# Four graph layers on one core: layer 3's transposes through DRAM rewritten, the last graph's end cut in two, and a new instruction order

## The chip, the cores and the metric

The kernel runs on one core of a Trainium2 chip. Its metric is the device time of one execution, in microseconds. The engines named below are TensorE (PE, with PEld for its weight loads), VectorE (DVE), ScalarE (ACT), GpSimd (POOL) and SyncE (SP), which here issues every DMA.

## The reference

There are 64 graphs of 256 tokens with 256 features each, and a 256 x 256 adjacency per graph, all in fp32. Four layers follow each other, and each ends with `x = layernorm(x + layer(x, adj))`.

```python
# layer 0: 4 heads of 64
X, q, k = lrelu(x @ W_lin + b_lin), lrelu(x @ W_q), lrelu(x @ W_k)      # slope 0.01, split into heads
adj_h = adj * sigmoid(q @ k.T / 8); deg = adj_h.sum(-1)
dis = where(deg > 0, deg ** -0.5, 0)
Y = (dis[:, None] * adj_h * dis[None, :]) @ X                           # then a layernorm with ln_g, ln_b
# layer 1: 8 heads of 32
q, k, v = x @ Wq + bq, x @ Wk + bk, x @ Wv + bv
out = softmax(where(adj > 0, q @ k.T / sqrt(32), NEG)) @ v              # per head, then @ Wo + bo
# layer 2
agg = epsilon * x + adj @ x
h = silu(rmsnorm(agg @ W1 + b1) * rms_weight)                           # 256 -> 1024
out = h @ W2 + b2
# layer 3: one head
Wh = x @ W; e = lrelu(Wh @ a1 [:, None] + Wh @ a2 [None, :])            # slope 0.2
h = softmax(where(adj > 0, e, NEG)) @ Wh
out = gelu(layernorm(h) * gamma + beta)
```

## The kernel before

**Tiles.** A tile has 128 partitions. A graph's 256 x 256 matrix is held as 128 x 512, two blocks of 128 rows side by side. An fp32 matmul of 128 x 128 weights with 128 x 256 data appears in the trace as a pair of PE instructions; a product of two 256 x 256 matrices takes four such matmuls. Heads use small tiles of TensorE: layer 0's scores (L550) have 64 rows, layer 1's (L631) 32 rows; layer 0's product AX (L590) fills 64 columns at a time, and layer 1's attention times values `av` (L667), the degrees `deg` (L568) and the mean of squares of layer 2 (L733) 32 columns. The planner calls these modes `rows` and `columns`, and the others `full` and `transpose`.

**One graph after another, interleaved.** The function `graph` writes down the operations of one graph. Each is recorded by `Plan.op` with its engine, a cost, the values that it reads and writes, a delay `after` until its result has landed, and, for a DMA, a size. `Plan.order` then runs a greedy list scheduler over the operations of all 64 graphs: it keeps a clock for each engine, and takes next the ready operation with the smallest key.

```python
key = start + LEAD[op.rank], op.due + RANK[op.rank], op.graph, op.index
```

`LEAD` and `RANK` have one number per operation of a graph, `CHANGE` is the cost of going from one PE mode to another, `STAY` and `TURN_STAY` bias against leaving the small-tile modes, `AHEAD` limits how early a graph starts, and `SLOTS` is the number of buffers of each kind. Activation tables are taken in turns (`ROUND`, `TAIL`), so that a graph's layer 1 runs two turns after its layer 0, and so on: several graphs are in flight, each in another layer. `JOINT` glues the mean-of-squares matmul of one graph to a score matmul of another. The engines' instructions are issued in the order that this plan gives; nothing is reordered on the chip.

**Transposes.** TensorE needs the contracted index on the partitions, so tokens and features change places several times. Most of these transposes go through DRAM: DVE transposes 32 x 32 blocks (L377), SP writes the tile to a DRAM buffer `far` (64 KB pieces at L383), and reads it back with the blocks in their new places (L387). Layer 0 uses the form with `in_order=False` (one write of 256 KB at L391, four reads at L393), layer 1 a similar one (L652 to L656), and layer 3 the form with `in_order=True`, twice a graph: for its input `xT3` and for its attention weights `eT`. In the first and last graphs (`NEAR`) TensorE transposes instead (L365), and one ACT copy of 128 x 512 (L412) brings the result out of PSUM.

**Layer 3 and the end.** The input is transposed, multiplied by the weights with two more columns for a1 and a2 (L770), copied (L774), and one of the extra columns is spread over the partitions as a row (`row_of`, L402 to L405: DVE and four POOL operations). ACT adds and applies the leaky relu (L778), the softmax is L513 on DVE and L518 on ACT, `eT` is the transposed weights, and `token_major` (L432) multiplies them with the values. Statistics are L445 to L457 with one power on POOL (L455); then L490 to L504 scale and shift, L789 is the gelu, L790 the sum with x, a second normalisation gives `o` (L464 to L472), and L792 writes 256 KB out. For the last three graphs (`ENDS`) ACT does part of the scaling (L493, L468).

Of the kernel before, what the change touches and what calls it, by code (L numbers as in the profile page):

```python
# [9 lines left out]
AF = mybir.ActivationFunctionType  # L10
# [19 lines left out]
AHEAD = 12.7  # L30
STAY, TURN_STAY = 197, 988
# [8 lines left out]
SLOTS = {"s": 42, "d": 10, "b": 3, "c": 72, "p": 8, "h": 8, "t": 5, "w": 3, "f": 8}  # L40
# [3 lines left out]
    3.44, -1.34, 0, 0.79, 3.63, 0, 7.06, 0, 0, 2.3, -1.09, 0.34, 2.1, 0.78, 0.47, 0, -8.07, 0, -2.5, 0, 15.95,  # L44
    3.93, 0.83, -0.82, -4.23, -2.95, 1.61, -7.35, 4.27, 6.06, 1.96, 5.09, -16.2, 5.57, 0.49, -0.6, 0, 0.29, 0.2,
    0, 8.07, 0, 0.26, 0, 0, -8.02, -0.52, 0.34, -5.71, 0, 1.06, -2.37, 0.99, -8.94, 0, 0, -4.56, -2.34, -6.61,
    0.36, 0.84, -1.13, 0.53, 4.6, -1.2, -1.71, 0, 0, 0, -0.62, 4.15, -3.45, -2.5, -0.12, 6.63, 0.18, 0, 0.38,
    -0.79, -2.84, 0, -12.65, 1.3, 0, -1.96, 1.34, -1.62, 20.11, -1.52, 0, -0.8, -2.32, -1.64, 0, -1.22, -15.66,
    0, -6.95, -2.98, 0, 0.05, -1.56, -0.82, -0.77, -6, -2.56, -2.91, -11.65, -5.25, -1.35, -5.62, 0.33, 0, 0.59,
    -0.44, -28.89, -6.83, 0, 0.4, 0, 0.46, 0.76, 0, 0, 12.94, -5.14, 4.78, 3.27, 0.41, -2.4, -1.34, 0, -0.87,  # L50
    -1.92, 0, -2.52, 0, -10.08, -2.01, 3.32, 0.57, -18.67, -3.41, 0, 4.56, 5.08, 3.05, -3.62, 0, 3.39, -0.48,
    -0.64, -0.1, -3.66, 19.76, -6.53, 16.91, 0, -3.84, -1.2, 0.37, -12.68, 0, -6.52, 5.03, 11.31, 6.22, 1.25,
    -5.4, 5.28, 9.76, 2.05, -0.81, -6.1, 0.74, -0.33, -6.78, -1.35, 0.27, 2.67, -2.73, 0.77, -0.98, -12.61, 0,
    1.81, 1.44, 1.4, -0.43, -5.6, 1.17, 0, -3.52, -0.14, -0.86, -0.05, -0.51, 0, 25.51, 0, 0, 0, -2.88, 0, 0, 0,
    -0.4, -0.07, 0, 0, 2.29, 0, 0, -2.22, -0.14, 1.6, 0.52, -0.32, -2.95, 0, 0, 0, -0.56, 0, -0.75, 8.73, 0, 0,
    0, 0.27, 9.58, -7, 0.78, 1.68, 0, -0.23, -10.25, -9.94, 0, 2.37, 3.11, -1.12, 0.31, -0.32, 0, -2.88, -2.04,
    0, -2.34, -0.49, -1.73, -1.73, -3.1, -1.77, 1.2, -3.97, 0.04, -0.58, -3.77, -19.26, 1.61, 0, 2.15, 0, 1.75,
    -9.45, 0, -11.3, -4.22, -40.55, -11.19, -1.7, 0, -1.02, 20.28, 2.54, 0, 0, -11.95, -3.71, 4.81, 4.78, 0, 1.6,
    0, 0, 0, -4.09, 0, -20.33, 0.55, 0.76, 0, 0, -5.26, 0.23, 2.23, 0.95, 0.44, -0.83, -0.57, -4.63, -0.68,
    -0.52, 11.56, 0.73, 0, 0, 5.95, 1.53, -1.94, 0, 1.27, 0.18, 0, -0.41, -3.03, -5.78, -1.03,  # L60
# [3 lines left out]
    0, 0, 0, 4, 0, 21, 963, 0, 0, 0, 63, 0, 36, -156, 0, 241, -51, 5, -54, -409, 0, 480, 0, -31, 0, 0, -1244, 5,  # L64
    0, 581, -13, 104, -75, 53, 0, 0, 0, 0, 0, 0, 0, 0, 0, 0, 0, 100, 0, 0, 0, 0, -88, -216, 0, -127, 0, 0, 0, 0,
    0, 0, 0, 0, 0, 0, 0, 0, 0, 0, 0, 0, 0, 73, 0, -648, -13, 0, 0, 0, 0, 0, 243, 0, 0, 0, 0, 0, 0, 52, 0, 0, 0,
    0, 0, 0, 0, 0, 0, -1022, -191, 0, 0, 0, -79, 0, 13, -157, 0, 0, 0, 0, 0, 0, 0, 0, 0, 0, 0, 0, 0, 0, 0, 0, 0,
    0, -14, -96, -46, -142, 175, -7, -49, -988, -8, 0, 0, 0, 0, -3, 56, -31, 223, 0, 72, -40, -885, 811, -10, 0,
    0, 0, 0, -181, 559, -5, 0, 0, 323, 144, 0, 239, -109, 0, 0, -40, 0, -97, -886, 230, 144, -105, 0, 2, -92, 38,
    -275, 0, 0, 0, 0, 0, -262, 0, 0, 0, -468, -319, 0, 0, 0, 0, -390, 256, 267, 0, 0, 0, 0, 0, 42, 0, 0, 0, 0, 0,  # L70
    -325, 0, 0, 0, 0, 0, -236, 0, -117, -279, 0, 0, -1, 0, 0, 0, 0, 0, 0, 0, 0, -14, 0, 0, 0, 0, 0, 0, 0, 0, 0,
    0, 0, 0, 0, 0, 0, -261, -256, 0, 0, 0, 0, 0, 0, 0, 0, -139, 0, 0, 37, 0, 0, 0, 0, 0, -156, 0, 0, 0, 0, 0, 0,
    0, 0, 0, -25, 0, 262, -10, 105, 0, 0, 0, 0, 0, -34, -107, -53, -189, -141, -364, 0, 0, -161, -46, -115, 0,
    -12, 0, -883, 0, 0, 0, 0, 0, 0, -109, -14, 0, 187, 0, -13, 721, 0, 0, -68, -68, 0, -58, 0, -31, 417, 0, 227,
]

# [40 lines left out]
class Plan:  # L117
# [66 lines left out]
    def order(self):  # L184
# [17 lines left out]
        while ready:  # L202
            best = None
            for op in ready:
# [10 lines left out]
                for kind, n in need.items():  # L215
                    free = self.free[kind]
                    if len(free) < n:
                        break
                    start = max(start, sorted(free)[n - 1][0])
                else:  # L220
                    key = start + LEAD[op.rank], op.due + RANK[op.rank], op.graph, op.index
                    if best is None or key < best[0]:
                        best = key, start, op
# [116 lines left out]
def graph(plan, nc, c, t, out, b):  # L340
# [14 lines left out]
    def load(name, src):  # L355
        v = Value("s", name, 2)
        op("SP", 470, lambda: nc.sync.dma_start(two(v), t[src][b].rearrange("(n p) d -> p n d", p=P)), [v], after=5000, size=256)
        return v
# [14 lines left out]
    def far_transposed(src, name, in_order=True):  # L373


        eb, far, dst = Value("s", "eb"), Value("h", "far", 4), Value("s", name, 4)
        op("DVE", 635, lambda: dve.transpose(  # L377
            eb.t.rearrange("p (b g i) -> p g b i", b=4, i=32),
            src.t.rearrange("p (n k w) -> p k n w", n=2, k=2)), [eb], [src])
        if in_order:  # L380
            F = lambda a: far.t[:64].rearrange("(a z) (y w) -> a (z y) w", a=4, w=P)[a]
            for a in range(4):
                op("SP", 470, lambda a=a: nc.sync.dma_start(  # L383
                    F(a).rearrange("(b j) w -> j b w", b=4),
                    eb.t[32 * a:32 * a + 32].rearrange("j (b w) -> j b w", b=4)), [(far, a)], [eb], after=2400, size=64)
            for a in range(4):
                op("SP", 655, lambda a=a: nc.sync.dma_start(  # L387
                    dst.t.rearrange("q (g a i) -> a q g i", g=4, a=4)[a],
                    F(a).rearrange("q (g i) -> q g i", g=4)), [(dst, a)], [(far, a)], after=2200, size=200)
            return dst  # L390
        op("SP", 470, lambda: nc.sync.dma_start(far.t[:, :512], eb.t), [(far, i) for i in range(4)], [eb], after=2900, size=256)  # L391
        for q in range(4):
            op("SP", 470, lambda q=q: nc.sync.dma_start(  # L393
                dst.t[32 * q:32 * q + 32].rearrange("j (a g) -> j a g", a=4),
                far.t[:, :512].rearrange("(a j) (b g) -> b j a g", a=4, b=4)[q]), [(dst, q)],
                [(far, i) for i in range(4)], after=1900, size=64)
        return dst

    def row_of(column, src, name):

        blocks, row = Value("t", "blocks"), Value("w", name, 4)
        op("DVE", 110, lambda: dve.transpose(  # L402
            blocks.t.rearrange("p (n k) -> p n k", n=NB), column().to_broadcast([P, NB, 32])), [blocks], src)
        for a in range(4):
            op("POOL", 300, lambda a=a: pool.partition_broadcast(  # L405
# [20 lines left out]
    def token_major(xT, w, r=()):  # L426

        ps = Value("p", "ps", 2)
        for n in range(NB):
            def fn(n=n):  # L430
                for k in range(DB):
                    pe.matmul(two(ps)[:, n, :], two(xT)[:, k, n * P:(n + 1) * P], w()[:, k, :],  # L432
# [7 lines left out]
    def stats(src, r=None):  # L440
# [13 lines left out]
        op("DVE", 300 if r else 60, fn, [mv], [mv] + [r] * bool(r))  # L454
        op("POOL", 720, lambda: pool.tensor_tensor(m()[:, :, 0], m()[:, :, 0], c.mhalf[:, :NB], OP.pow), [mv], [mv], after=400)  # L455
# [71 lines left out]

    xT, adjT, x, adj = load("x0T", "xT"), load("adjT", "adjT"), load("x", "x"), load("adj", "adj")
# [43 lines left out]
    op("DVE", 340, lambda ps=ps: dve.transpose(pd.t[:, :N], ps.t[:, :N]), [pd], [ps])  # L572
# [3 lines left out]
    op("POOL", 1610, lambda: pool.tensor_tensor(dp.t[:, :8], dp.t[:, :8], c.mhalf, OP.pow), [dp], [dp])  # L576
# [20 lines left out]
    else:  # L597
        yb = far_transposed(ps, "yT", in_order=False)
# [25 lines left out]
    for hq in range(H1 // 4):  # L624
# [9 lines left out]
        for pair in range(2):  # L634
# [20 lines left out]
            for q in range(4):  # L655
                op("SP", 470, lambda far=far, eT=eT, q=q: nc.sync.dma_start(  # L656
# [17 lines left out]
    op("DVE", 110, lambda: dve.transpose(  # L674
        rT.t.rearrange("p (n k h) -> p n k h", n=NB, h=H1),
        r.t[:, :16].rearrange("p (n h) -> p n h", n=NB)[:, :, None, :].to_broadcast([P, NB, 4, H1])), [rT], [r])
    op("SP", 470, lambda far=far: nc.sync.dma_start(far.t, rT.t), [far], [rT], after=2000, size=32)
    for h in range(H1):
        op("SP", 470, lambda h=h, far=far: nc.sync.dma_start(
            two(rb)[h % 4 * HD1:(h % 4 + 1) * HD1, h // 4, :].rearrange("p (a m) -> p a m", a=4),  # L680
            far.t.rearrange("(a c) m -> c a m", a=4)[h][None].to_broadcast([HD1, 4, 64])),
            [(rb, h)], [far], after=2000, size=40)
# [55 lines left out]
    op("DVE", 125, lambda ps=ps: dve.transpose(pm(), ps.t[:, :64]), [(sq, 1)], [ps])  # L738
    op("DVE", 50, lambda: dve.tensor_scalar(  # L739
        rs.t[:, :NB], pm().rearrange("p (n k) -> p n k", k=32)[:, :, 0], 1e-6, None, op0=OP.add), [rs], [(sq, 1)])  # L740
    op("POOL", 700, lambda: pool.tensor_tensor(rs.t[:, :NB], rs.t[:, :NB], c.mhalf[:, :NB], OP.pow), [rs], [rs])  # L741
# [19 lines left out]
    xT3 = copy(transposed(x), "xT3") if b >= plan.graphs - NEAR[2] else far_transposed(x, "xT3")  # L761
# [3 lines left out]
    for n in range(NB):  # L765
        ps = Value("p", "ps")

        def fn(ps=ps, n=n):
            for k in range(DB):
                pe.matmul(ps.t[:, :D + 2], two(xT3)[:, k, n * P:(n + 1) * P], c.w3.t[:, k, :],  # L770
# [6 lines left out]
    for n in range(NB):  # L777
        op("ACT", 360, lambda n=n: act.activation(two(e)[:, n, :], s2.t, AF.Prelu, bias=s1(n), alpha=0.2),  # L778
# [104 lines left out]
```

## Time and profile before

| what | value |
|---|---|
| median of 3 runs | 2665.98 us (2665.81 to 2669.04) |
| the profiled execution | 2665.97 us, its span 2664.2 us |
| PE busy | 2629.6 us, 99% |
| DVE busy | 2463.8 us, 92% |
| ACT busy | 2246.5 us, 84% |
| POOL busy | 640.5 us, 24% |
| share of the 16 DMA engines taken by packets | 69.7% |
| TensorE clock granted, mean | 0.996 of full speed |

The span is the time from the first to the last instruction in the trace; what is outside it is the difference to the profiled execution's own time. "Busy" is the time in which an engine carries out instructions. A wait is charged to the engine that waited, with what released it. A period is the distance between the same work of two consecutive graphs; 64 of them overlap.

### The profile page before, as it was taken

The numbers are of one execution on the slowest core, as the hardware profiler recorded it, in microseconds if no ns is written. First come the engines' busy times: TensorE is split into PE (matmuls) and PEld (weight loads), VectorE is DVE, ScalarE is ACT, GpSimd is POOL, SyncE is SP. The second block draws the span as 40 slices with busy tenths as digits, with TensorE's granted clock in tenths as the row PEclk, the third lists the DMA queues.
The fourth block names the chain that finished last, engine by engine and source line by source line (L and its number), as shares of the span: only waits on it lengthen the run. The fifth ranks groups of instructions, "written<-read, shape, count | busy, mean of one in ns | idle before, by whom it ended". The sixth has DMA issues, their size and how long they took to land.

```text
span 2664.2 us, 54927 instructions
## 1 busy us (share of the span) xinstructions
PE 2629.6 (99%) x17248; PEld 2122.6 (80%) x17248; DVE 2463.8 (92%) x6905; ACT 2246.5 (84%) x5343; POOL 640.5 (24%) x1029
## 2 busy tenths in 40 slices
PE   8999999999999999999999999999999999999997
PEld 6777888888887888888888878878888887877786
DVE  6799999999999999999999999999999999989976
ACT  4888888888888888988888888889889888888886
POOL 1122222222222222222222222222222222222222
PEclk9999999999999999999999999999999999999998
DMA  4577777776777777777767777777677776676761
GB/s 142 153 210 199 196 206 188 200 202 182 210 195 187 197 200 192 200 189 200 200 187 206 196 186 202 196 188 200 193 195 203 188 199 183 178 198 186 212 162 38
DMA packets 764628, 502.48 MB, mean 189 GB/s; under 512 B 383792, under 2 KB 724144, under 8 KB 764336
## 3 DMA queue, kind: packets, MB, share of 16 engines
q1 hardware_dynamic: 764336, 498.97, 69.7%
q8 instruction: 137, 2.24, 0.4%
q14 instruction: 155, 1.27, 0.2%
HBM read 301.35 MB, written 197.39 MB: 187 GB/s over the span
## 4 chain that ended last, share of the span: by engine, by line
PE 89%; DVE 5%; DMA 2%; SPq 1%; issue 1%; ACT 1%; POOL 1%; POOLq 0%; DVEq 0%; ACTq 0%
PE ps L432 16%; PE ps L755 15%; PE ps L421 15%; PE ps L714 15%; PE ps L631 5%; PE ps L702 4%; PE ps L550 4%; PE ps L590 4%; PE av L667 4%; PE ps L770 4%; PE ps L365 1%; PE ps L568 1%; DVE mv L445 1%; DVE e L513 1%; DMA eT<-far 1%
## 5 line engine op out<-in xcount | busy, mean ns | idle before, releaser
L518 ACT ACTIVATE e<-e,low 128x256 f32<-128x256 f32 x1152 | 576.4, 503 | 156.9 <-DVE low L513 150.9
L455 POOL TENSOR_TENSOR mv<-mv,mhalf 128x2 f32<-128x2 f32 x384 | 313.7, 822 | 965.7 <-DVE mv L453 759.8
L714 PE MATMUL ps<-aggT,w 128*128 128x256 f32 x2048 | 463.8, 379 | 0.0
L755 PE MATMUL ps<-w,hT 128*128 128x256 f32 x2048 | 456.4, 380 | 0.0
L755 PEld LDWEIGHTS ps<-w,hT 128*128 128x128 f32 x2048 | 387.8, 190 | 56.1 <-issue 2.7
L714 PEld LDWEIGHTS ps<-aggT,w 128*128 128x128 f32 x2048 | 387.3, 190 | 56.6 <-issue 1.9
L513 DVE CUSTOM_DVE_ANT_0 e<-ps,adj 128x256 f32<-128x256 f32 x1024 | 361.9, 418 | 29.7 <-PE ps L631 28.1
L652 DVE STREAM_TRANSPOSE eb<-e 128x1024 f32<-128x1024 f32 x248 | 305.2, 1232 | 2.5 <-ACT e L518 0.4
L721 ACT ACTIVATE hT<-ps,br,r 128x256 f32<-128x256 f32 x512 | 259.5, 576 | 1.8 <-PE ps L755 0.9
L719 ACT ACTIVATE sq<-ps,b 128x256 f32<-128x256 f32 x512 | 218.2, 469 | 24.1 <-PE ps L714 23.9
L468 ACT ACTIVATE x<-y,mv 128x256 f32<-128x256 f32 x384 | 215.4, 595 | 18.2 <-DVE mv L464 18.1
L518 ACT ACTIVATION_READ_ACCUMULATOR e<-e,low 128x1 f32 x1152 | 220.8, 192 | 0.0
L445 DVE BATCH_NORM_STATS2 mv<-y 128x6 f32<-128x512 f32 x320 | 217.3, 692 | 0.6
L556 DVE TENSOR_TENSOR att<-att,adjT 128x512 f32<-128x512 f32 x256 | 164.7, 682 | 9.1 <-ACT att L554 8.9
L741 POOL TENSOR_TENSOR rs<-rs,mhalf 128x2 f32<-128x2 f32 x64 | 45.4, 709 | 521.2 <-DVE rs L739 519.8
L576 POOL TENSOR_TENSOR dp<-dp,mhalf 128x8 f32<-128x8 f32 x64 | 126.6, 1978 | 161.6 <-DVE dp L575 161.3
L745 DVE TENSOR_TENSOR hT<-hT,pr 128x1024 f32<-128x1024 f32 x128 | 149.1, 1202 | 2.2 <-POOL pr L405 2.1
L631 PE MATMUL ps<-kT,qT 32*128 32x256 f32 x2048 | 147.8, 400 | 0.0
L554 ACT ACTIVATE att<-ps 128x512 f32<-128x512 f32 x256 | 138.8, 600 | 3.9 <-PE ps L550 3.2
L726 DVE TENSOR_TENSOR sq<-sq 128x512 f32<-128x512 f32 x192 | 130.9, 682 | 9.1 <-ACT sq L719 8.8
L421 PE MATMUL ps<-x0T,w_k 128*128 128x256 f32 x512 | 131.9, 385 | 6.1 <-DMA w_k<-in_L_gnn_W_k 6.1
L747 ACT ACTIVATE hT<-hT 128x1024 f32<-128x1024 f32 x128 | 133.3, 1051 | 3.4 <-DVE hT L745 2.7
(116 smaller groups left out, 5460.9 us busy)
## 6 DMA issues: line engine op xcount, KB each, us to landing
far<-eb SPq DMA_DIRECT2D x248, 512.0 KB, 3.1
eT<-far SPq DMA_DIRECT2D x992, 128.0 KB, 4.1
adj<-in_adj SPq DMA_DIRECT2D x128, 256.0 KB, 5.8
far<-eb SPq DMA_DIRECT2D x488, 64.0 KB, 2.4
x<-in_x SPq DMA_DIRECT2D x64, 256.0 KB, 5.1
x0T<-in_xT SPq DMA_DIRECT2D x64, 256.0 KB, 5.0
adjT<-in_adjT SPq DMA_DIRECT2D x64, 256.0 KB, 5.5
adj<-in_adjT SPq DMA_DIRECT2D x64, 256.0 KB, 5.6
```

What stands on the lines that cost most here:

```text
L421: pe.matmul(two(ps)[:, o, :], w.t[:, k, o * P:(o + 1) * P], two(xT)[:, k, :], start=(k == 0), stop=(k == DB - 1))
L432: pe.matmul(two(ps)[:, n, :], two(xT)[:, k, n * P:(n + 1) * P], w()[:, k, :], start=(k == 0), stop=(k == DB - 1))
L445: op("DVE", 615, lambda: dve.bn_stats(mv.t[:, :6], src.t[:, :512].rearrange("p (n c) -> p c n", n=NB)), [mv], [src])
L455: op("POOL", 720, lambda: pool.tensor_tensor(m()[:, :, 0], m()[:, :, 0], c.mhalf[:, :NB], OP.pow), [mv], [mv], after=400)
L513: op("DVE", 345, lambda n=n: dve.tensor_tensor_reduce(out=E(n), in0=two(logits)[:, n, :], in1=two(negmask)[:, n, :], scale=-scale, scalar= ...
L518: op("ACT", 491, lambda n=n: act.activation(E(n), E(n), AF.Exp, bias=low.t[:, n:n + 1], scale=-1.0, accum_out=r.t[:, col(n):col(n) + 1]), ...
L631: pe.matmul(two(pss[i])[:, n, :], two(qT1)[s, hq, n * P:(n + 1) * P], two(kT1)[s, hq, :], start=True, stop=True)
L652: op("DVE", 1155, lambda e=e, eb=eb: dve.transpose(eb.t.rearrange("p (b g i) -> p g b i", b=4, i=32), e.t.rearrange("p (g b i) -> p g b i" ...
L714: pe.matmul(two(ps)[:, i, :], c.w2_1.t[:, k, (j + i) * P:(j + i + 1) * P], two(aggT)[:, k, :], start=(k == 0), stop=(k == DB - 1))
L719: op("ACT", 357, lambda ps=ps, sq=sq, i=i, j=j: act.activation(two(sq)[:, i, :], two(ps)[:, i, :], AF.Square, bias=c.b2_1.t[:, j + i:j + i ...
L721: op("ACT", 491, lambda ps=ps, i=i, j=j: act.activation(Hb(j + i)[:, 0], two(ps)[:, i, :], AF.Identity, bias=c.br2.t[:, j + i:j + i + 1], ...
L755: pe.matmul(two(ps)[:, n, :], Hb(j)[:, 0, n * P:(n + 1) * P], c.w2_2.t[:, j, :], start=(j == 0), stop=(j == HB - 1))
```

## The change

- `far_transposed` keeps only the form of layer 0. A new `far_shuffled` does layer 3's two trips: one write of 256 KB instead of four of 64 KB, and four reads, all in pieces of 256 bytes. The tokens of the result alternate: token n * 128 + i of the graph stands in column 2 * i + n.
- The matmuls that read such a result (L770, and the one with `eT`) take every second column as weights (`ordered_block`).
- `near` takes the place of one copy by two, which write with the same stride, in the last three graphs.
- The last graph's end is written in two halves of 128 tokens each (`last`).
- The planner's numbers are replaced: costs and landing delays of SP, POOL and some DVE operations, `AHEAD`, `STAY`, `TURN_STAY`, `SLOTS`, `RANK` and `LEAD`; a table `LIKING` adds a bias for each pair of PE modes to the first part of the key. The order of all instructions on every engine follows from them.

```diff
-AHEAD = 12.7
-STAY, TURN_STAY = 197, 988
+AHEAD = 12.6
+STAY, TURN_STAY = 287, 390
-SLOTS = {"s": 42, "d": 10, "b": 3, "c": 72, "p": 8, "h": 8, "t": 5, "w": 3, "f": 8}
+SLOTS = {"s": 44, "d": 10, "b": 3, "c": 36, "p": 8, "h": 8, "t": 5, "w": 3, "f": 8}
...
+LIKING = {("rows", "columns"): -23, ("rows", "transpose"): 23, ("columns", "full"): 82, ("columns", "rows"): -167, ("columns", "columns"): -2, ("columns", "transpose"): 128, ("transpose", "rows"): -81, ("transpose", "columns"): 83}
...
-                    key = start + LEAD[op.rank], op.due + RANK[op.rank], op.graph, op.index
+                    lead = LEAD[op.rank] + (LIKING.get((mode, op.mode), 0) if op.engine == 'PE' else 0)
+                    key = start + lead, op.due + RANK[op.rank], op.graph, op.index
...
-        if in_order:
-            F = lambda a: far.t[:64].rearrange("(a z) (y w) -> a (z y) w", a=4, w=P)[a]
-            for a in range(4):
-                op("SP", 470, lambda a=a: nc.sync.dma_start(
-                    F(a).rearrange("(b j) w -> j b w", b=4),
-                    eb.t[32 * a:32 * a + 32].rearrange("j (b w) -> j b w", b=4)), [(far, a)], [eb], after=2400, size=64)
-            for a in range(4):
-                op("SP", 655, lambda a=a: nc.sync.dma_start(
-                    dst.t.rearrange("q (g a i) -> a q g i", g=4, a=4)[a],
-                    F(a).rearrange("q (g i) -> q g i", g=4)), [(dst, a)], [(far, a)], after=2200, size=200)
-            return dst
...
+    def far_shuffled(src, name):
+        eb, far, dst = Value("s", "eb"), Value("h", "far"), Value("s", name, 4)
+        op("DVE", 635, lambda: dve.transpose(
+            eb.t.rearrange("p (b k i n) -> p k n b i", b=4, k=2, n=NB),
+            src.t.rearrange("p (n k b i) -> p k n b i", n=NB, k=2, b=4)), [eb], [src])
+        F = lambda: far.t[:64].rearrange("(b k r) (p m) -> b k (r p) m", b=4, k=2, m=64)
+        op("SP", 470, lambda: nc.sync.dma_start(
+            F().rearrange("b k p m -> p (b k) m"), eb.t.rearrange("p (g m) -> p g m", m=64)), [far], [eb], after=2900, size=220)
+        for q in range(4):
+            op("SP", 590, lambda q=q: nc.sync.dma_start(
+                dst.t[32 * q:32 * q + 32].rearrange("j (g m) -> j g m", m=64),
+                F()[q].rearrange("k (a j) m -> j (k a) m", a=4)), [(dst, q)], [far], after=2800, size=64)
+        return dst
+
+    def near(src, name):
+        ps, dst = transposed(src), Value("s", name, 2)
+        for k in range(DB):
+            op("ACT", 357, lambda k=k: act.copy(
+                two(dst)[:, k, :].rearrange("p (i n) -> p n i", n=NB),
+                two(ps)[:, k, :].rearrange("p (n i) -> p n i", n=NB)), [(dst, k)], [ps])
+        return dst
+
+    def ordered(ap):
+        return ap.rearrange("p (i n) -> p n i", n=NB)
+
+    def ordered_block(ap, n):
+        return ordered(ap)[:, n]
...
-                pe.matmul(ps.t[:, :D + 2], two(xT3)[:, k, n * P:(n + 1) * P], c.w3.t[:, k, :],
+                pe.matmul(ps.t[:, :D + 2], ordered_block(two(xT3)[:, k, :], n), c.w3.t[:, k, :],
...
+    def last(n, eT, v3, V3, r, x):
+        ps, st, y, o = Value("p", "ps"), Value("c", "mv"), Value("w", "y"), Value("w", "o")
...
+                pe.matmul(ps.t[:, :D], ordered_block(two(eT)[:, k, :], n), V3()[:, k, :D], start=(k == 0), stop=(k == DB - 1))
+        op("PE", 2 * PE_MM, fn, [ps], [eT, v3])
...
+        op("DVE", 328, lambda: dve.bn_stats(st.t[:, :6], ps.t[:, :D]), [st], [ps])
...
+        op("ACT", 322, lambda: act.activation(y.t, y.t, AF.Gelu), [y], [y], turn=turn(3, GELU))
+        op("DVE", 345, lambda: dve.tensor_tensor(y.t, y.t, two(x)[:, n, :], OP.add), [y], [y, x])
...
+        op("DVE", 328, lambda: dve.tensor_scalar(
+            o.t, y.t, mean(), root(), op0=OP.subtract, op1=OP.mult), [o], [y, st])
+        op("SP", 470, lambda: nc.sync.dma_start(out[b].rearrange("(n p) d -> p n d", p=P)[:, n, :], o.t), [], [o], after=2300, size=128)
...
+    eT = near(e, "eT") if b >= plan.graphs - NEAR[2] else far_shuffled(e, "eT3")
+    if b == plan.graphs - 1:
+        for n in range(NB):
+            last(n, eT, v3, V3, r3, x)
+        return
+    ps = token_major(eT, lambda: V3()[:, :, :D], [v3], ordered_block)
```

## Prediction

> **What bounds the kernel now.** I read the table of busy times first, then the stretches, then TensorE's waits, then the timeline of one graph and of the end.
>
> ```profile
> PE 2629.6 (99%) x17248; PEld 2122.6 (80%) x17248; DVE 2463.8 (92%) x6905; ACT 2246.5 (84%) x5343; POOL 640.5 (24%) x1029
> ```
> ```profile
> 266.00:1332.00 1066.00, 1066.00 (x7035) 866.25 (x7037) 1015.54 (x2837) 916.41 (x2174) 260.99 (x419) 1.00 0.73 197
> ...
> 2636.00:2664.20 28.20, 10.02 (x44) 7.36 (x44) 19.56 (x61) 15.69 (x35) 8.23 (x13) 0.72 0.11 38
> ```
> Columns of a stretch: its length, then busy time of PE, PEld, DVE, ACT and POOL, granted clock, DMA share, GB/s. From 266 to 1332 us (and on to 2250) PE is never idle, with DVE at 95% just behind it. In the last 28 us PE has nearly nothing to do and DVE works 19.56.
>
> ```profile
> PE ps L421 <- DMA w_k<-in_L_gnn_W_k: 6.1, 1, 6.1
> PE ps L365 <- ACT x L468: 3.2, 3, 2.6
> PE ps L432 <- ACT eT L412: 1.9, 1, 1.9
> PE ps L770 <- DMA xT<-far: 1.9, 2, 1.1
> ```
> These are the largest waits of the whole span. In 266 to 2250 us the list is empty. So the transfers of layer 3, which the change rewrites, hold PE up for 1.9 us (xT) and 0.7 us (eT) in all, and only in the drain.
>
> ```profile
> 1627.80 1.95 PE L590 MATMUL ps<-att,v 128*64 128x256 f32 x16
> 1629.67 0.32 PE L733 MATMUL ps<-sq,mean_of 128*32 128x64 f32 x8
> 1629.92 1.15 PE L631 MATMUL ps<-kT,qT 32*128 32x256 f32 x16
> 1631.00 1.99 PE L702 MATMUL ps<-adj,x 128*128 128x256 f32 x8
> ...
> 1633.79 1.15 PE L631 MATMUL ps<-kT,qT 32*128 32x256 f32 x16
> 1634.86 1.99 PE L432 MATMUL ps<-v,eT 128*128 128x256 f32 x8
> ...
> 1654.07 2.00 PE L550 MATMUL ps<-qT,kT 64*128 64x256 f32 x16
> 1656.00 1.93 PE L667 MATMUL av<-eT,v 128*32 128x256 f32 x32
> 1657.75 0.62 PE L568 MATMUL ps<-added,ones 128*32 128x128 f32 x16
> ```
> One graph's small-tile matmuls, in three clusters: AX, mean, scores; scores; att, av, deg. A graph takes 40.64 us (L421 w_k at 1622.52 and again at 1663.15).
>
> The profiled execution is 2665.97 us, its span 2664.2, so 1.8 lies outside; the median is 2665.98. Of the span, PE is dense (back to back) for 2622.9; it waits 6.1 at the start, and stalls 19.5 between: 8.7 before 300 us (1.8 of it half-clock matmuls at the start), 5.9 in 2300 to 2460, 4.6 in 2634 to 2648, 0.3 elsewhere. About 15.7 lies after its last matmul. A change can move only PE's dense time, the stalls and the end.
>
> **Part 1, the trips.** Per graph and trip it replaces 4 writes (128 packets of 512 B each) and 4 reads (512 of 128 B) by one write and 4 reads with 1024 packets of 256 B each way. Packet durations in the trace: 128 B 12.9 ns, 256 B 18.0, 512 B 31.3. Before: 512 x 31.3 + 2048 x 12.9 = 42.4 us of one DMA engine, 2.65 over 16; after: 2048 x 18.0 = 36.9, 2.30. SP issues 8 writes at 433 ns and 8 reads at about 600 a graph = 8.3 us; after, 2 writes at 562 (L391's row) and 8 reads at 600 = 5.9. All of this lies off the path: no PE wait names it in steady state. Gain there: 0. In the drain it can return at most the 2.6 us above. Nearly all the 256 B packets I priced are the reads of rb; writes of 256 B could cost up to the 31.3 of a 512 B packet, 2.0 instead of 1.15 us per write, still off the path. [...]
>
> The tokens now alternate, so DVE's transpose (L377, 671 and 687 ns) writes with a stride of two elements, and 8 matmuls a graph (L770's and the last L432's) load weights with that stride. No weight load in this trace is strided. Bounds: below, nothing (no reason for a gain); above, half rate. A load's record lasts 190 ns, and loads follow each other every 216 ns, so 26 ns are to spare; at half rate 380 ns would stand against 216, 164 ns x 1024 loads (8 x 2 passes x 64) = +168 us. I take 0, the nearest row being the same load with unit stride; I keep the other end as a rival. [...] DVE has 2.0 us per graph to spare (95% of 40.64); two transposes at half rate would take 1.36 of them.
>
> The near copies of the last three graphs (L412, 584 ns for 128x512) become two of 128x256, about 0.43 each by the 376 ns of L774's 128x258: 0.3 more, six times, of which two (the last graph's) lie on the path: +0.5, inside the end's sum.
>
> **Part 2, the planner's new order: dense time.** The number of matmuls is unchanged, 8798. What moves is how small-tile blocks stand next to each other. Start-to-start intervals in the trace price this: full after full 432 ns a pair of instructions; entering another tile shape +93; the first full matmuls after one +104. Blocks alone, with the entry: mean 342 ns, scores 1169 (two a graph), AX 1970, att 2021, av 1957, deg 667; sum 9295. Where two small-tile blocks touch, the leaving cost of the first merges: 93 saved, but 231 where both have 32-column tiles (av next to deg or mean). Before: AX-mean 93, mean-scores 93, att-av 93, av-deg 231: 9295 - 509 = 8786. The instruction order of the changed program has in most graphs the clusters mean, scores; scores, AX, deg; att, av: four joins at 93, 9295 - 372 = 8923. That is +0.14 us per graph, some 46 graphs: +6.5. At both ends the new order joins more than the old. Counted over the whole order (joins at 93: 167 before, 224 after; at 231: 55 and 11; returns to full tiles 218 and 202) the same prices give 2619.6 for the old order, 3.3 below its measured 2622.9, and 2623.0 for the new: **+3.4**. The join scores-AX (47 times) is unseen; 93 is its nearest row, 231 the other end (-6.5), nothing saved the worst (+4.4).
>
> **Part 2, stalls.** Each hop between two PE blocks through ACT, DVE, POOL or a transfer has a shortest time (trace) and the PE time that the order puts between. Where before stalled in the ramp the new order gives more: AX of graph 1 to its transpose 25.2 us against 22.1 (needs 24.7), scores 2 to av 56.3 against 38.6 (40.3). New tight ones: features to scores of graph 1, 1.5 against a need of 2.6, and of graph 0, 2.1; scores 0 to its transposes 10.1 to 10.6 against 10.8 to 12.3. I make the ramp 3.4 to 6 us of stalls instead of 6.9, and let the drain lose 1 to 2 of its 5.9 with the longer transfer times the plan now assumes: **-4**, between -13 (nearly all reducible stalls gone) and +10. In steady state the smallest hops: av to its token matmul 1.92 (needs 0.95), w1_o to agg 7.5 instead of 10.9 (needs 5.1 at its shortest, 7.5 with the queue that DVE has today), agg to W1 1.7 instead of 4.1 (needs 0.8). None is negative, so no steady stall.
>
> **Part 3, the end in halves.** The last graph's final chain is cut by token half, each with its own stats, power, two scalar-tensor ops, gelu, add, norm and output. The timeline of the end:
>
> ```profile
> 2643.96 0.49 ACT L518 ACTIVATE e<-e,low 128x256 f32<-128x256 f32 x1
> ...
> 2658.61 0.70 POOL L455 TENSOR_TENSOR mv<-mv,mhalf 128x2 f32<-128x2 f32 x1 [2.63 <-DVE mv L453]
> 2659.35 0.16 DVE L464 SCALAR_TENSOR_TENSOR mv<-mv 128x2 f32<-128x2 f32 x1 [0.81 <-POOL mv L455]
> 2659.55 1.09 ACT L468 ACTIVATE o<-y,mv 128x256 f32<-128x256 f32 x2 [1.69 <-DVE mv L464]
> ```
> From the last softmax op on DVE (ends 2643.81) to DVE's end at 2659.51 are 15.7 us, and the durations of its instructions there add up to 15.3: graphs 61 and 62 still have their ends too, and DVE is the limit, not latency. The same stretch in the new order, priced by these rows (128x256 pieces 0.36 to 0.47 where 128x512 take 0.68, short ops 0.15 to 0.18 twice): 17.9, +2.6. Behind it stand ACT's normalisations of graphs 61 and 62 (4 x 0.55 instead of 2, +1.1), released 0.4 before DVE's end: +2.6 - 0.4 + 1.1 = **+3.3**, I take +3. If DVE were not the limit, a half as the last link would shorten the chain by about 3 (half of gelu, add, stats, norm and the output): -3.
>
> **Sum.** 2664.2 + 3.4 + 3 - 4 = 2666.6, and 1.8 outside: 2668.4, say **2668**. Within 0.2% (5.3 us, about what a measurement can tell from no change) of 2665.98.
>
> **Rivals.** (a) Stalls gone: the order is fitted to transfers as traced, and -13 is there to be had; with the halves at -3 to +3: 2665.98 + 3.4 - 13 ± 3, about 2656, or 2650 if the scores-AX join is worth 231. For it: nearly every place that stalled is relaxed. Against: the new tight hops of the ramp. Chance 0.29. (b) A steady stall: w1_o to agg at 7.5 leaves nothing over today's loaded time; from the point where DVE's queue before that norm is no shorter than now, PE waits. 0.25 us x 47 graphs = +12: 2680. For it: DVE is at 95% and this hop lost 3.4 us. Against: the reorder may put that norm first. Chance 0.24. (c) A worse end and drain (+4 and +4 over the sum): 2676, chance 0.08. (d) Strided weights that cost: 2836 at half rate (2668 + 168), 2752 if half of that; chance 0.05. Mine: 0.34.
>
> The range leaves 0.1 below and about 0.1 above: 2653 to 2685. Faster 0.29, same 0.34, slower 0.37.
>
> **What would show it.** PE's wait list empty from 300 to 2250 us (else b, with L702 in it); a period of about 40.78 us; LDWEIGHTS of L770's line still 190 ns (else d); no wait on a layer-3 transfer; the last softmax to DVE's end about 18 us; ramp stalls near 5 us. A period under 40.6 or an end under 30 us from the last W2 matmul (32.2 now) would prove me wrong.

## The result, and the profile after

Over 20 runs each, the changed kernel takes 2670.76 us at the median and the kernel before 2665.13; the ratio is 1.0021, with a 95% interval of 1.0015 to 1.0027. That is 5.6 us or 0.21% slower: inside the range, 2.8 us above the forecast, and on the edge of what was called no change. The profiled execution after is 2672.62 us with a span of 2670.8, 6.6 more than before.

The busy times and two of the stretches (same columns as before):

```profile
PE 2636.1 (99%) x17248; PEld 2127.7 (80%) x17248; DVE 2433.3 (91%) x6919; ACT 2254.9 (84%) x5346; POOL 609.9 (23%) x1031
```
```profile
266.00:1332.00 1066.00, 1066.00 (x6970) 865.00 (x6970) 997.33 (x2830) 920.29 (x2176) 245.31 (x418) 1.00 0.69 197
...
2636.00:2670.80 34.80, 15.61 (x69) 12.03 (x67) 23.30 (x81) 17.45 (x44) 10.70 (x19) 0.79 0.14 44
```
PE is again never idle in the middle, but in 1066 us it gets through 6970 instructions instead of 7035. The count is a sign and not a measure: it falls by 0.9%, the period below grows by 0.3%, and small-tile blocks have many short instructions (16 in 1.15 us below, where full tiles have 8 in 2.00). One graph's small-tile blocks in the timeline of PE say what became dearer:

```profile
1632.93 0.32 PE L797 MATMUL ps<-sq,mean_of 128*32 128x64 f32 x8
1633.18 1.15 PE L695 MATMUL ps<-kT,qT 32*128 32x256 f32 x16
1634.25 2.86 PE L778 MATMUL ps<-aggT,w 128*128 128x256 f32 x12
1637.04 1.15 PE L695 MATMUL ps<-kT,qT 32*128 32x256 f32 x16
1638.12 1.95 PE L654 MATMUL ps<-att,v 128*64 128x256 f32 x16
1639.99 0.65 PE L632 MATMUL ps<-added,ones 128*32 128x128 f32 x16
1640.57 2.00 PE L456 MATMUL ps<-v,eT 128*128 128x256 f32 x8
...
1657.20 2.00 PE L614 MATMUL ps<-qT,kT 64*128 64x256 f32 x16
1659.12 1.93 PE L731 MATMUL av<-eT,v 128*32 128x256 f32 x32
1660.99 1.99 PE L456 MATMUL ps<-w_l,x0T 128*128 128x256 f32 x8
```
deg (L632) now follows AX (L654) instead of av (L731). From entry to exit (from the start of the last full pair before a cluster, less that pair's 432 ns, to the start of the first full one behind it) the three clusters take 1418, 3621 and 3885 ns at the median; the prediction's prices made them 1418, 3620 and 3885. So the unseen join of scores and AX saved 93. The median period is 40.78 us, as forecast, against 40.64.

The waits of PE in the whole span, the largest:

```profile
PE ps L445 <- DMA w_k<-in_L_gnn_W_k: 6.1, 1, 6.1
PE av L731 <- DVE low L537: 2.9, 1, 2.9
PE ps L559 <- ACT eT L412: 1.9, 1, 1.9
PE ps L632 <- DVE added L626: 1.1, 1, 1.1
```
The ramp's old stall at 64.8 us (2.8) is down to 0.8, but av of graph 3 now waits 2.9 us at 177. From 266 to 2250 us the list is empty here too.

To compare kernels, each trace is split at places in it. "Dense" is PE's time from its first matmul to the start of the last W2 matmul less the stalls; a stall is what a block takes over its price in the prediction's rows (rounding included, so that a number may be a little below nothing). "End" runs from the start of the last W2 matmul (its last pair of instructions) to the end of the span. What is left of a span is the wait for `w_k` before the first matmul, 5.6 to 6.5 us. All in us, one profiled execution each:

| kernel | span | dense | stalls to 60 | 60 to 133 | 133 to 266 | 266 to 2250 | 2250 to W2 | end |
|---|---|---|---|---|---|---|---|---|
| before | 2664.2 | 2607.0 | 1.9 | 5.9 | 3.3 | -0.1 | 7.2 | 32.8 |
| changed | 2670.8 | 2610.5 | 2.1 | 2.5 | 6.2 | 0.2 | 8.8 | 34.5 |
| e1 old trips | 2689.6 | 2610.4 | 1.9 | 1.7 | 3.4 | 2.7 | 28.6 | 34.3 |
| e2 old end | 2675.4 | 2610.4 | 2.5 | 1.6 | 10.5 | 0.0 | 8.3 | 35.9 |
| e3 before, new trips | 2665.3 | 2607.0 | 3.0 | 5.8 | 3.4 | 0.2 | 6.5 | 33.1 |
| e4 before, deg apart | 2682.4 | 2623.1 | 2.1 | 5.4 | 6.4 | 0.2 | 6.2 | 33.1 |
| e5 changed, deg rejoined | 2657.8 | 2604.2 | 2.2 | 1.8 | 2.4 | 0.1 | 7.9 | 33.7 |
| e6 changed, ready steps first | 2669.2 | 2610.6 | 2.0 | 1.3 | 5.2 | 0.9 | 9.0 | 34.0 |
| e7 before, trips and halves | 2657.5 | 2607.0 | 2.2 | 4.6 | 2.8 | 0.0 | 3.1 | 31.9 |

The dense column repeats to 0.2 us among kernels with one order on PE; the stalls differ by several us between executions, and single runs of one kernel lie 7 to 10 us apart (the profiled execution of e5 is 5.8 us below its kernel's median, that of e7 3.5 below, that of e2 2.8 above). So medians of many runs decide on a kernel, and the table only says where.

Of the 6.6 us between the first two rows, 3.5 are dense, about 1.5 stalls and 1.7 the end. By the medians of 20 runs, 5.6 us, the dense time and the end leave only some 0.4 for the stalls.

### The profile page after: what moved, and what is told of

The parts are those of the page before. It is cut to its first block, busy times and chain, and to the rows that moved or that the text cites. A ratio compares the mean times of both kernels' runs of the same rounds, so it can differ in the third digit from the quotient of the medians.

```text
span 2670.8 us, 54753 instructions
## 1 busy us (share of the span) xinstructions
PE 2636.1 (99%) x17248; PEld 2127.7 (80%) x17248; DVE 2433.3 (91%) x6919; ACT 2254.9 (84%) x5346; POOL 609.9 (23%) x1031
## 4 chain that ended last, share of the span: by engine, by line
PE 91%; DVE 5%; ACT 1%; DMA 1%; POOL 1%; SPq 1%; issue 1%; ACTq 0%; DVEq 0%; POOLq 0%
PE ps L778 16%; PE ps L819 16%; PE ps L445 15%; PE ps L456 15%; PE ps L695 5%; PE ps L654 4%; PE ps L614 4%; PE ps L766 4%; PE av L731 4%; PE ps L834 4%; PE ps L370 1%; PE ps L632 1%; DVE e L537 1%; PE ps L797 1%; DVE eb L716 0%
## 5 line engine op out<-in xcount | busy, mean ns | idle before, releaser
L778 PE MATMUL ps<-aggT,w 128*128 128x256 f32 x2048 | 470.3, 382 | 1.4 <-ACT att L618 0.9
L716 DVE STREAM_TRANSPOSE eb<-e 128x1024 f32<-128x1024 f32 x248 | 299.8, 1211 | 2.3 <-ACT e L542 1.4
L785 ACT ACTIVATE hT<-ps,br,r 128x256 f32<-128x256 f32 x512 | 269.7, 569 | 26.2 <-PE ps L654 26.2
L618 ACT ACTIVATE att<-ps 128x512 f32<-128x512 f32 x256 | 132.9, 603 | 3.1 <-PE ps L614 2.4
L445 PE MATMUL ps<-x0T,w_k 128*128 128x256 f32 x512 | 125.0, 384 | 6.1 <-DMA w_k<-in_L_gnn_W_k 6.1
L614 PE MATMUL ps<-qT,kT 64*128 64x256 f32 x1024 | 128.5, 389 | 0.2 <-DVE yT L749 0.2
```

The costliest lines, as they stand in the source:

```text
L445: pe.matmul(two(ps)[:, o, :], w.t[:, k, o * P:(o + 1) * P], two(xT)[:, k, :], start=(k == 0), stop=(k == DB - 1))
L614: pe.matmul(two(pss[2 * hp + i])[:, m, :], two(kT)[s, hp, m * P:(m + 1) * P], two(qT)[s, hp, :], start=True, stop=True)
L716: op("DVE", 1155, lambda e=e, eb=eb: dve.transpose(eb.t.rearrange("p (b g i) -> p g b i", b=4, i=32), e.t.rearrange("p (g b i) -> p g b i" ...
L778: pe.matmul(two(ps)[:, i, :], c.w2_1.t[:, k, (j + i) * P:(j + i + 1) * P], two(aggT)[:, k, :], start=(k == 0), stop=(k == DB - 1))
L785: op("ACT", 491, lambda ps=ps, i=i, j=j: act.activation(Hb(j + i)[:, 0], two(ps)[:, i, :], AF.Identity, bias=c.br2.t[:, j + i:j + i + 1], ...
```

## The experiments

The planner is chaotic: another count of operations gives another order everywhere. To change one thing alone, the experiments plan twice: once as the file does, and a second time, with the experiment's operations, by the start that each operation had in the first plan. In the traces the order of TensorE's matmuls in e1 and e2 is that of the changed kernel to the instruction, and in e3 and e7 that of the kernel before. The edits below show what takes effect; the switch by which one file plans both versions is left out.

```diff
+            if target:
+                best = self.next_by(target, ready, clock)   # the ready op, with tiles free, of the smallest target[op.key]
...
+    target = {op.key: op.start for op in first_plan.order()}
```

**e1: the new order with the old trips.**

```diff
-    xT3 = near(x, "xT3") if b >= plan.graphs - NEAR[2] else far_shuffled(x, "xT3")
+    xT3 = near(x, "xT3") if b >= plan.graphs - NEAR[2] else far_transposed(x, "xT3")     # in order: four writes, four reads
...
-        return ordered(ap)[:, n]
+        return ap[:, n * P:(n + 1) * P]
...
-                two(dst)[:, k, :].rearrange("p (i n) -> p n i", n=NB),
+                two(dst)[:, k, :],
```


> The changed kernel with layer 3's trips as before (four writes and four reads in order, unit stride for the transposes, the near copies and the weights); every other instruction of every engine stands in the changed kernel's order, and the order on TensorE is the same to the instruction. Theory (the loss is the dense time of TensorE and the end; the trips are off the path): within 2 us of the changed kernel, 2669 to 2673. Rival (the new trips cost: pieces of 256 bytes, weights and transposes with stride): the loss goes away, 2667 or less. Second rival (the new trips pay, the order is what costs): clearly above 2673, since the new order leaves the transfers less time.

Measured: 2693.66 us, ratio to before 1.0099 (1.0086 to 1.0112). The second rival: under the new order the new trips are worth about 21 us by the ratios (the medians are 22.9 apart, but the kernel before was itself 1.3 slower in that series). The waits of PE show what the old ones do there:

```profile
PE ps L497 <- DMA eT<-far: 12.4, 6, 5.3
...
PE ps L875 <- DMA xT<-far: 2.7, 3, 1.7
```
L497 is `token_major` behind the trip of eT. 28.6 us of stalls lie in the drain, and 1.7 of the waits in the middle, where neither kernel has any. For the largest wait, 5.27 us before PE's L497 at 2348.68, the timeline of SP tells SP's issues and the landing apart. DVE has the transposed block ready at the same time in both, 2330.8. First the changed kernel, then e1, each with its write and the last read of that trip:

```profile
2332.22 0.40 SPq L400 DMA_DIRECT2D far<-eb  x1
2339.45 0.43 SPq L403 DMA_DIRECT2D eT<-far  x1
...
2334.55 1.86 SPq L429 DMA_DIRECT2D far<-eb  x4
2344.65 0.52 SPq L433 DMA_DIRECT2D eT<-far  x1
```
The last read goes out 5.2 to 5.3 us later, and PE's matmul starts 5.4 later (2343.24 in the changed kernel). From the end of that issue to the matmul it is 3.4 and 3.5 us. So here SP's issuing is late, not the landing: SP has four writes instead of one, and a read takes it 0.63 us at the median instead of 0.45. From 266 to 2250 us SP spends 67% of its time issuing transfers in e1, and 58% in the changed kernel. The other waits were not taken apart. The old trips are off the path only in the order that was made for them.

**e2: the new order with the end in one piece.**

```diff
-    if b == plan.graphs - 1:
-        for n in range(NB):
-            last(n, eT, v3, V3, r3, x)
-        return
```


> The changed kernel with the last graph's end in one piece; everything else in the changed kernel's order. Theory: the two traces have 32.4 and 34.0 us from the last W2 matmul to the end, so 1.6 us of the loss are the halves: 2669, between 2667.5 and 2670. Rival (the halves do shorten the chain and only the order before them is worse): 2671 to 2674.

Measured: 2674.36 us, 1.0027 (1.0017 to 1.0038), against 1.0021 of the changed kernel; the intervals overlap. The trace says where: the end is 35.9 us against 34.5. So the halves save about 1.4, the rival's side. It may be too much: each whole piece was placed where the second half's step had stood, an order that was not made for it. The timeline of e2's end shows what the whole pieces wait for:

```profile
2659.79 1.93 ACT L547 ACTIVATE y<-ps,mv 128x256 f32<-128x256 f32 x4 [4.34 <-DVE mv L544]
2661.75 0.69 DVE L550 TENSOR_TENSOR y<-y,g 128x512 f32<-128x512 f32 x1 [1.45 <-ACT y L547]
...
2668.36 3.06 ACT L522 ACTIVATE o<-y,mv 128x256 f32<-128x256 f32 x6 [1.76 <-DVE mv L518]
```
DVE stands idle for 1.45 us behind ACT, and three normalisations of 128x512 (six instructions) queue on ACT at the very end.

**e3: the old order with the new trips.**

```diff
-    xT3 = copy(transposed(x), "xT3") if b >= plan.graphs - NEAR[2] else far_transposed(x, "xT3")
+    xT3 = near(x, "xT3") if b >= plan.graphs - NEAR[2] else far_shuffled(x, "xT3")
...
-    eT = copy(transposed(e), "eT") if b >= plan.graphs - NEAR[2] else far_transposed(e, "eT3")
-    ps = token_major(eT, lambda: V3()[:, :, :D], [v3])
+    eT = near(e, "eT") if b >= plan.graphs - NEAR[2] else far_shuffled(e, "eT3")
+    ps = token_major(eT, lambda: V3()[:, :, :D], [v3], ordered_block)
```


> The kernel before with the new trips alone (one write, alternating tokens, two near copies), in the old order on every engine. Theory: no change, 2665 +- 1.5 us; TensorE's period stays 40.64 us, the weight loads with stride take about 196 ns as in the changed kernel. Rival (the trips cost): 2668 or more. Rival (they pay): 2662 or less.

Measured: 2664.77 us, 0.9992 (0.9983 to 1.0000): 1.7 us less than before at the median, between a gain and nothing. The new trips themselves cost nothing that can be measured.

**e4: the price of a neighbour.**

```diff
+    for a, deg, full in zip(pe, pe[1:], pe[2:]):        # pe: TensorE's steps of the first plan
+        if a.key[1] == ("av",) and deg.key[1] == ("deg",) and full.mode == "full":
+            target[deg.key] = full.start + 1
```


> The kernel before with one PE step moved: the degree matmuls (deg), which stand behind av in 48 graphs, come one full-tile step (two matmuls, 0.86 us) later. The same work. Theory (TensorE has no slack, and neighbours set the price): each loses the join of two 32-column blocks, 231 ns, and a second return to full tiles, 104 ns: 0.335 us x 48 = +16.1, about 2681. Rival (TensorE's time is hidden behind DVE, at 95%): within 3 us of before.

Measured: 2684.20 us, 17.7 more than before at the medians; ratio 1.0064 (1.0051 to 1.0077). The dense time is 16.1 us longer and the period 40.97 us; the moved step and the cluster that it left take 335 ns more a graph at the median, as priced. One step of 0.67 us, moved by one step, with the same work on every engine: the neighbours alone make the difference, and nothing hides it.

**e5: the new order with deg back behind av.**

```diff
+    for i, deg in enumerate(pe):
+        if deg.key[1] == ("deg",) and pe[i - 1].key[1] == ("AX",):
+            av = next((op for op in pe[i + 1:i + 60] if op.key[1] == ("av",)), None)
...
+            target[deg.key] = av.start + 1
+            for n, after in enumerate((2900, 3400, 3500, 5500, 6500)):       # its steps on DVE and POOL
+                key = deg.graph, ("dg",), n
+                target[key] = max(target[key], target[deg.key] + after)
```


> The changed kernel with the degree matmuls moved back behind av: in 46 graphs deg leaves the place behind AX (a join at 93 ns) for the one behind av (231 ns), some 21 us later, and its five small steps on DVE and POOL follow it. Theory (neighbours on TensorE make the dense part of the loss): 0.139 us x 46 = 6.4 us less than the changed kernel, about 2664.5. Rival (the shorter way from deg to AX, 17 us instead of 38, and the other order on DVE make new stalls): 2669 or more.

Measured: 2665.38 us, 0.9998 (0.9989 to 1.0007): 0.23% below the changed kernel's ratio, about 6 us. Dense time fell from 2610.5 to 2604.2. The timeline of PE shows the join again: deg starts 1.76 us after av, where in the changed kernel the next full block started 1.87 after it.

```profile
1649.30 1.93 PE L758 MATMUL av<-eT,v 128*32 128x256 f32 x32
1651.06 0.62 PE L659 MATMUL ps<-added,ones 128*32 128x128 f32 x16
1651.61 1.99 PE L483 MATMUL ps<-w_l,x0T 128*128 128x256 f32 x8
```
The period is 40.64 us again. That one move is worth as much as the whole loss of the changed kernel. It is not the whole cause of it: the move gives back 6.3 us of dense time where the change had lost 3.5, so that dense time now lies 2.8 below that of before, and this makes up for the rest.

**e6: ready steps ahead of stalled ones.**

```diff
+EARLIER = [(134, [135, 136, 137]), (2422, [2423, 2424, 2425]), (58, [59]), (174, [180, 182])]   # TensorE's steps by number
+    for i, earlier in EARLIER:
+        for n, j in enumerate(earlier):
+            target[pe[j].key] = pe[i].start - 1 + 0.01 * n
```


> The changed kernel with four stalled TensorE steps behind two or three steps that were ready: c1 before a transpose of graph 0 at 63 us, three steps before deg at 133, two before av of graph 3 at 177, three before the features of graph 63 at 2535. Theory (the rest of the loss is single hops of the ramp and the drain that the new order made too short): the stalls at these places, 0.8 + 1.25 + 4.6 (with the half clock that follows) + 1.1 = 7.7 us in the profiled execution, go down by 4 to 5: about 2666. Rival (a stall that is taken away comes back at the next hop): 2670 or more.

Measured: 2671.35 us, 1.0013 (1.0004 to 1.0022): perhaps 2 us less than the changed kernel, with overlapping intervals. Of the four places, the waits at 63 and 133 us are gone, the one at 177 went from 2.9 to 2.0, and the stall at 2535 stayed at 1.07; at 68 and 142 us waits of 0.8 came up where 0.3 had been. Neither theory holds whole: part of a stall that is filled returns at the next hop. The 177 us place proves little either way, since it varies without any edit (see the stalls below).

**e7: the old order with trips and halves.**

```diff
+    if b == plan.graphs - 1:
+        for n in range(NB):
+            last(n, eT, v3, V3, r3, x)                    # each step at the place of the whole one
+        return
```


> The kernel before, in its own order, with the new trips and with the last graph's end in halves. Against the kernel with the new trips alone (ratio to before 0.9992). Theory A (DVE is the limit in the end, and the halves add 2.4 us of work there): 2 us more, ratio 0.9999. Theory B (as in the changed kernel, where the whole end was 1.5 us longer from the last matmuls to the end): 1.5 us less, ratio 0.9986.

Measured: 2662.81 us, 0.9985 (0.9976 to 0.9994): theory B by the number, though its interval overlaps that of e3. The end is 31.9 us against 33.1 of e3, and that repeats: e9, with halves, has 31.8, e4 and e8, without, 33.1 each. The last instruction on DVE in e7:

```profile
2653.83 0.93 DVE L628 TENSOR_SCALAR o<-y,mv 128x256 f32<-128x256 f32 x2 [0.38 <-POOL mv L603]
```
DVE writes the result itself, with a wait of 0.4. In e3 DVE waits 0.8 for POOL, and then ACT's 1.09 us follow.

**e8 and e9: the old order with three ramp stalls filled, and with everything.**

```diff
+EARLIER = [(231, [232, 233]), (116, [117, 118]), (167, [168])]
```


> The kernel before, in its own order, with the new trips, and three stalled TensorE steps of the ramp (AX of graph 4 at 120 us, av of graph 3, the features of graph 6 at 243) behind one or two steps that were ready. Theory: 2 us less than with the new trips alone, ratio to before 0.9985. Rival: no change, 0.9992.

> The kernel before in its own order with all that paid in single runs: the new trips (0.9992), the last graph's end in halves (0.9985 with the trips), and the three ramp steps behind ready ones (0.9984 with the trips). Theory (the three gains lie at different places and add up: -1.7, -1.9, -2.0 us): ratio to before 0.9978, some 2660.5. Rival (a stall taken from the ramp is given back later): 0.9985 or more.

Measured: e8 2662.24 us, 0.9984 (0.9975 to 0.9993); e9 2662.77 us, 0.9986 (0.9977 to 0.9995). e8's trace does not show the gain where it was meant: the stalls to 266 us are 11.0 together, against 12.2 of e3, and the drain has 3.1 instead of 6.5, which the edit does not touch. At 120 us the wait of 1.2 for AX is gone, but the step behind it waits 2.1 for yT. e9 brought nothing over e7 or e8, as the rival said. e7, e8 and e9 are each faster than both kernels, by 0.15% than before. Among the three there is no difference that these runs show; e7 is the one whose gain, 1.2 us in the end, shows where its edit is.

## Why the prediction was right, and where its steps failed

**Dense time: right to the tenth.** +3.4 was forecast and 3.5 came; the prices of neighbours carried over to clusters that the trace of before did not have. e4 (16.1 forecast, 16.1 in the dense column) and e5 (6.4 forecast, 6.3) show it as a cause: moving one step to other neighbours moves the time by the sum of the prices. It is 3.5 of the 5.6 us.

**Stalls: the term "-4" did not come.** They are 19.8 against 18.2 us in the two traces, and by the medians only some 0.4 apart. From 60 to 133 us the places that were relaxed did relax (5.9 to 2.5). But av of graph 3, which was not on the list of new tight hops, waits 2.9 us at 177. From the end of its scores to av the order before has 39.5 us, with no wait for av; the new one has 40.2 with the 2.9, so 37.3. How much of this belongs to the order is not shown: with the same order on TensorE av waits 0.5 us there in e1 and 4.7 in e2. The drain, 2250 us to W2, was to fall by 1 to 2. It is 8.8 instead of 7.2, and it lies higher in the new order throughout (7.9 to 9.0 in the changed kernel, e2, e5 and e6; 3.1 to 7.2 in the old order). Why was not tested.

**The end: right in sign, wrong in cause.** +3 was forecast for the halves, with DVE as the limit. In the trace the end is 1.7 longer, but the halves shorten it: by 1.4 in the new order (e2 against the changed kernel) and 1.2 in the old one (e3 against e7). The step that failed is "DVE is the limit, not latency". It rests on durations that add up to 15.3 of 15.7 us, but the rows overlap: 21 of the 37 behind the first start before the one ahead of them ends, by 0.08 us at the median. The busy time of the stretch in the kernel before, from 2643.81 to the end of the span, says 13.76 (the third busy time):

```profile
2643.81:2664.20 20.39, 3.46 (x12) 2.09 (x12) 13.76 (x40) 9.97 (x20) 5.05 (x7) 0.61 0.15 51
```
So DVE had 1.9 us of gaps up to its end, 1.5 of them waits for POOL and ACT. (The 15.7 us that the prediction puts behind the last matmul are 14.6 by the timeline, where it ends at 2649.6; no term hangs on that.) In e7 it has more to do than in e3 (15.4 us busy from the last softmax to the end, 13.4 in e3), but the waits shrink (0.4 us in e7, 2.2 in e3, PE's matmuls included), and it ends 0.35 later after the last softmax. The 1.1 us of ACT behind DVE fall away, and the last write, 128 KB instead of 256, ends 2.7 us after the last instruction instead of 3.2.

What makes the changed kernel's end longer is the order: from the last softmax to the end it takes 22.2 us, and e7, with the same halves, 19.4. Of the 2.8, 0.6 is DVE's later end, 1.2 is ACT behind it and 1.0 the last write, which is a whole one again. The lines of the changed kernel show what stands last:

```profile
2664.94 2.08 ACT L492 ACTIVATE o<-y,mv 128x256 f32<-128x256 f32 x4 [2.68 <-DVE mv L488]
2665.43 0.41 DVE L588 TENSOR_SCALAR o<-y,mv 128x256 f32<-128x256 f32 x1 [0.52 <-POOL mv L563]
```
The last half is out of DVE at 2665.84, and ACT still normalises graphs 61 and 62 until 2667.02. Four normalisations instead of two came as forecast, but they start 0.9 us before DVE's end and not 0.4. So ACT adds 1.2 behind DVE, where before had 1.1, and not the 0.7 more of the sum; DVE's end is 1.6 later and not 2.2 (17.3 us after the last softmax, 15.7 before).

**The trips: "gain 0, off the path" held in the old order only.** e3 bears it out (0 forecast, -1.7 with an interval that reaches nothing). But the change is trips and order together, and in the new order the old trips cost some 21 us. The reading was made against an order that was being replaced, and it gave no value to SP's issue time, on which the 21 us hang at least in part. That time was also put too high for the new trips: a read takes 0.45 us and not 0.6, a write 0.36 and not 0.56, so a graph's ten issues take 4.3 us at the medians and not 5.9. The open price of a 256-byte write is settled by the trace after: its packets of 256 bytes, the trips' writes among them, last 18.0 ns on average, as priced, and not the 31.3 that the prediction left open. The sign "no wait on a layer-3 transfer" came nearly true: 0.7 us for eT in the drain, where before had 2.6.

**The rivals.** (a) did not come: the stalls were not removed. (b), a steady stall, did not come: no wait from 266 to 2250 us, and w1_o to agg at 7.5 us was enough. (d), weights with stride, is settled by the groups of the changed kernel:

```profile
L834 PEld LDWEIGHTS ps<-w,xT 128*128 128x128 f32 x512 | 99.9, 196 | 12.5 <-ACT xT L412 1.0 <-issue 0.4
```
196 ns instead of 190, still inside the 216 between loads. It shows behind a small-tile cluster: the first full pair takes 544 ns from start to start when it loads strided weights, and 536 otherwise. So the stride adds 6 ns to a load, where half rate would have added 190. DVE's transposes with stride take 699 and 704 ns instead of 671 and 687, also small.

(c), a worse end and drain by 4 us each, did not come as such, though both moved its way.

By the spans, the sum fell 4.2 us short of the 6.6: the stalls were put about 5.5 too low, the end 1.3 too high, the dense time 0.1 too low. The profiled execution after lies 1.9 us above its kernel's median, the one before 0.8, so the medians come out closer, at 5.6 against a forecast of 2.4. That the total lies so near is luck in part: two of the three terms had errors, and these went opposite ways. One of the three was right for its reason.

## What to carry to other kernels

When an engine is busy throughout, ask what its work costs in that order, not only what it waits for: the start-to-start prices of neighbours on TensorE, read from one trace, gave the new order's dense time to 0.2 us, and one moved step per graph was worth 6 us. Judge an edit in the order that it will run in; a transfer that nothing waited for in one order cost some 21 us in another (e1), where at its largest wait the queue that issues it came 5 us late. Before calling one engine the limit of a tail, take its busy time and not the sum of its rows, which overlap, and look for what it waits for: short waits there were room for more, smaller pieces (e7, 1.2 us).

## What the runs showed of the hardware

In the changed kernel one wait costs more than its length: av waits 2.9 us, and the matmuls behind it are slow too (stretches of the changed kernel; the granted clock is the third number from the end):

```profile
170.00:176.80 6.80, 4.01 (x43) 2.83 (x42) 6.80 (x34) 5.00 (x19) 0.00 (x0) 1.00 0.85 220
176.80:180.00 3.20, 3.11 (x33) 2.32 (x33) 0.79 (x5) 0.00 (x0) 0.69 (x1) 0.65 0.00 0
180.00:181.50 1.50, 1.50 (x5) 1.27 (x6) 1.50 (x7) 0.00 (x0) 0.76 (x2) 0.61 0.00 0
181.50:184.00 2.50, 2.50 (x13) 2.22 (x12) 1.67 (x4) 2.26 (x8) 1.71 (x1) 1.00 0.17 67
```
The clock is full during the wait; in narrower stretches it is 0.50 from 178 to 181 us. av and the four instructions behind it take 3.00 and 1.59 us from start to start. In e6 av waits 1.96 us at the same place, the clock stays at 1.00, and they take 1.98 and 0.97: so the drop costs 1.6 us on top of the wait. In the kernel before, where TensorE waits 2.65 us until 64.8, the clock is 0.50 too, from 64.4 to 67.8. So it fell at these waits of 2.65 and 2.88 us, and did not at the one of 1.96.

In these kernels small-tile blocks took less time side by side than apart. av and deg, both 32 columns wide, save 231 ns (before, e3, e5), and blocks of unlike tiles save 93, also scores and AX, which stand side by side in the new order only. Entering a small-tile block from full tiles costs 93 ns, and the first full pair behind it 104 on top of its 432, in both kernels.
